# Where a convolution stage takes its spectrum's sign and mean, in which banks its last unit works, and in which order its first unit is built

## The chip, the cores and the metric

The kernel runs on one core of one Trainium2 chip. The metric is the device time of one execution in microseconds. Before the change it was 3066.25 us, the median of 3 runs (3065.99 to 3067.99).

## What is computed

The input `x` has 8 images of 32 channels of 256 x 256. Four layers follow one another, each of the form `x = x + layer(groupnorm(x))`. Only the first two matter here, and the normalisation between them:

```python
# _gn: mean and variance over pairs of channels of one image
# layer 0: a Fourier layer: 64 x 32 modes are mixed over channels, then inverted
x_ft = jnp.fft.rfft2(x)
out_lo = jnp.einsum('bixy,ioxy->boxy', x_ft[:, :, :M1H, :M2H], w1)
out_hi = jnp.einsum('bixy,ioxy->boxy', x_ft[:, :, -M1H:, :M2H], w2)
...
out = jnp.fft.irfft2(out_ft, s=(h, w))
x = x + (out + bias)
# layer 1: one 5 x 5 filter, the same for all channels
x = x + conv5x5(_gn(x))
```

Layers 2 and 3 are a recurrence over the columns and a mix of directional maxima; the change does not touch them.

## The kernel before

The program has four stages, one after another: `forward_and_mix` (forward transform and mixing of modes, which leaves the mixed spectra in the DRAM tensor `smd`), `inverse_and_conv` (inverse transform, residual sum, 5 x 5 convolution, which leaves layer 1's result in the DRAM tensor `x2d`), `recurrence` and `maxima_and_mix`. All the change lies in `inverse_and_conv` (L297 to L664). That stage starts at about 295 us and ends at about 1034 us of the profiled execution.

**Units.** The stage works on 16 units `u`. A unit is half an image, 16 channels; two units share one image `b` and so one spectrum. A unit's channels are held as two halves `ch`, each of 4 groups, so a unit has 8 groups `g`. The loop from L614 runs over units and, inside, over groups. The order in each engine's queue is the order in which this loop issues instructions, since the whole stage is under a manual schedule; nothing reorders it.

**What one unit needs before its convolution.** These steps run for unit u+1 and u+2 in between the groups of unit u:

- `load_spectrum(b)` (L345): three DMAs bring a spectrum from `smd` to a tile `spec`. From the third image on they are issued from ScalarE's queue, in odd units after group 2 (L652).
- `spectrum(b)` (L355): VectorE negates one half of the tile (L358, 64 x 1024 elements in place), TensorE takes the mean of the image with one matmul into a bank `y0` (L360, two passes), and six small VectorE instructions (L362 to L372) turn that mean into a correction of the spectrum's row 0 (L371) and into statistics. It is called for image 0 before the loop, for image 1 in unit 0 after group 2 (L635), and for images 2 to 7 in odd units 1, 3, 5, 7, 9 and 11 after group 5 (L654).
- `over_rows(u, c)` (L394): four matmuls (L401, recorded as 8) into a bank `tp`, then a ScalarE copy into SBUF (L408). Inside the loop these run after groups 3 to 6 for unit u+2.
- `over_columns` through `transform(u, p)` (L410, L579): matmuls of one of 9 column blocks `p` into two banks `up` (L418, recorded as 16), then two VectorE sums with the input into the tiles `x1` (L427). After blocks 2, 5 and 8 GpSimd issues the loads of the next unit's input (L379). There are five tiles `x1`, used in turn by halves of units, so block 0 of unit u+2 writes to tiles that held the last half of unit u-1 and the first half of unit u.
- `squares` (L435): sums of squares per group, by ScalarE (L444) or, where told, VectorE (L440). `scale(u, ch)` (L446): matmuls of these sums (L451), one VectorE instruction (L455), and a power by GpSimd (L457), which gives the factor `r` that the convolution's results of that half are multiplied with.

**The convolution of a group** (`conv`, L469): 18 matmuls (L487, recorded as 36) into three banks `vp`, then five VectorE instructions (L520) that multiply the banks by `r` and add them to `x1` in place, then ScalarE's squares (L527). After a half of a unit, `store` (L534) writes it to `x2d` by 12 DMAs from the queue of SyncE (for the last half of all, half of them from ScalarE's). `statistics(u-1)` (L550) after group 2 takes the sums over partitions with four matmuls (L556, recorded as 8) into a bank, then four VectorE instructions (L564 to L568) and a GpSimd power (L569).

**Banks.** The eight banks of PSUM are shared out by tag: `vp` has 4, `up` has 3, `st` has 1. The one bank `st` serves `y0`, `tp`, the sums of `scale` and those of `statistics` in turn: each has to wait until the one before has been read. A group of `conv` takes 3 of the 4 `vp` banks.

**The start of the stage** (L594 to L613): after the first spectrum, `over_rows` of unit 0 uses `st` and `up` in turn; then the 9 blocks of unit 0 are built with the `vp` banks, and `over_rows` of unit 1 stands after blocks 1, 3, 5 and 7, always in the bank `st`. The squares of blocks 5 to 8 are taken by ScalarE for half 0 and by VectorE for half 1. `scale(0, 1, 3)` comes next in TensorE's queue, then block 0 of unit 1, then unit 0's convolution with `scale(0, 0, 3)` within its first group.

**The end of the stage.** In the last unit there is nothing left to transform; only conv groups, their squares and two small sums remain. The next stage begins with a transpose of statistics (L707) into SBUF that the stage's tiles have held.

Of the kernel before, what the change touches and what calls it, by code (L numbers as in the profile page):

```python
# [16 lines left out]
P = 128  # L17
# [10 lines left out]
NT = 9  # L28
# [268 lines left out]
def inverse_and_conv(tc, k, d, smd, xmean, x2d, stb, first):  # L297
# [13 lines left out]

    PLACES = (1, 2, 3, 5, 6, 7, 8)
    with ExitStack() as ctx:
        one = ctx.enter_context(tc.tile_pool(name="a2c", bufs=1))
# [39 lines left out]

        def spectrum(b):  # L355

            t = specs[b]
            nc.vector.tensor_scalar_mul(t[64:128, :, 1], t[64:128, :, 1], -1.0)  # L358
            y0 = ps.tile([P, C], F32, name=f"y0_{b}", tag="st")
            nc.tensor.matmul(y0, lhsT=k.dc, rhs=t[:, :, 0, 0], start=True, stop=True)  # L360
            yb = sm.tile([P, C], F32, name=f"yb_{b}", tag="yb")
# [107 lines left out]
        def conv(u, ch, g, between=()):  # L469
# [3 lines left out]


            vps = [
                ps.tile([P, 2 * (hi - lo), Q], F32, name=f"vp_{u}_{ch}_{g}_{lo}", tag="vp", bufs=4) for lo, hi in BANKS
            ]
# [71 lines left out]

        def statistics(u):  # L550
            b, h = units[u]
            s1 = state.pop(u)["s1"]
            n8 = 2 * G
            sp = ps.tile([P, 2, n8], F32, name=f"s2_{u}", tag="st")
            for n in range(4):
                nc.tensor.matmul(  # L556
                    sp,
                    lhsT=k.valid[:, 2 + min(n, 2), :],
                    rhs=s1[:, :, n].rearrange("p k c g -> p k (c g)"),
                    start=n == 0,  # L560
                    stop=n == 3,
                )
            st = sm.tile([P, 2, n8], F32, name=f"st2_{u}", tag="st2")
            nc.vector.tensor_copy(st, sp)  # L564
            ve = sm.tile([P, n8], F32, name=f"ve2_{u}", tag="ve2")
            nc.vector.tensor_tensor(ve, st[:, 0], st[:, 0], ALU.mult)
            nc.vector.tensor_tensor(ve, st[:, 1], ve, ALU.subtract)
            nc.vector.tensor_scalar(ve, ve, 0.0, EPS, ALU.max, ALU.add)  # L568
            nc.gpsimd.tensor_tensor(st[:, 1], ve, k.mhalf[:, :n8], ALU.pow)  # L569
            return st  # L570

# [21 lines left out]
        with tc.manual_schedule(engines=None):  # L593
            load_spectrum(0)  # L594
            load_spectrum(1)
            for i in range(3):
                load(0, i)
            spectrum(0)
            for u in range(2):
# [3 lines left out]
            for p in range(NT):  # L603
                transform(0, p)
                if p % 2:
                    over_rows(1, p - 1)
                if p == 4:
                    for ch in range(2):
                        squares(0, ch, 1, 1, 5)
            for ch in range(2):  # L610
                squares(0, ch, 2, 5, NT, ch == 1)
            scale(0, 1, 3)
            transform(1, 0)  # L613
            for u in range(n):  # L614
                more, beyond = u + 1 < n, u + 2 < n
                for g in range(2 * G):
# [10 lines left out]
                    if g == 2 * G - 1 and beyond:  # L627
                        transform(u + 2, 0)
                    if g == 1 and u > 0:
                        scale(u, 1)  # L630
                    if g == 2:
                        if u > 0:
                            st = statistics(u - 1)
                        elif beyond:
                            spectrum(units[u + 2][0])  # L635
                    if g == G - 1 and beyond:
# [3 lines left out]
                    if g == 6 and more:  # L640
                        squares(u + 1, 0, 2, 8, NT)
                    squares2(u, g // G, g % G)
                    if g == 1 and more:
                        for ch in range(2):
                            squares(u + 1, ch, 0, 0, 1)
# [4 lines left out]
                    if u % 2 and u + 3 < n:  # L650
                        if g == 2:
                            load_spectrum(units[u + 3][0])  # L652
                        elif g == 5:
                            spectrum(units[u + 3][0])  # L654
                    if g % G == G - 1 and (u, g) != (n - 1, 2 * G - 1):
# [544 lines left out]
```

## Time and profile before

| | before |
|---|---|
| median of 3 runs | 3066.25 us |
| profiled execution | 3069.01 us |
| its span | 3067.2 us |
| TensorE busy over the span | 2796.5 us (91%) |
| VectorE busy | 2585.2 us (84%) |
| ScalarE busy | 1870.4 us (61%) |
| GpSimd busy | 858.2 us (28%) |

Times inside the profiled execution are counted from the start of its span. In lines of the timeline, the columns are start in us, length in us, engine, source line, operation, the tile written and the tiles read, shape, count, and in square brackets how long the engine sat idle before it and what ended that. One row may merge many instructions of one kind. In lines of windows, the columns are the window, its length, then for each engine the busy us and the number of instructions, then granted TensorE clock, DMA share and GB/s.

Almost all of the stage's time lies between the first and last L520 instruction, 357.29 and 1021.18 us, and can be cut into units there: a unit's length is taken from the start of its first L520 instruction to that of the next unit's. Read so from the timeline of VectorE, the lengths of units 0 to 14 are 40.49, 42.31, 41.35, 45.51, 41.35, 45.55, 41.35, 45.48, 41.35, 42.31, 41.35, 42.31, 41.35, 41.35 and 37.59 us.

### The profile page before, as it was taken

How to read it: one execution, taken by the hardware profiler on the slowest of the kernel's cores; microseconds unless marked ns; L12 is line 12 of the kernel's file. 1: busy time of each engine (PE TensorE's matmuls, PEld its weight loads, DVE VectorE, ACT ScalarE, POOL GpSimd, SP SyncE). 2: the span in 40 equal slices, each digit the busy share in tenths (PEclk: the TensorE clock that was granted, in tenths of full speed). 3: DMA queues.
4: the chain of work that ended last, by engine and by line, in shares of the span. 5: the costliest groups of instructions: out<-in, count | busy, mean ns of one | idle time of the engine just before them, and what ended most of it. 6: DMA issues, size and time to landing. Idle time of an engine off the chain costs nothing.

```text
span 3067.2 us, 111686 instructions
## 1 busy us (share of the span) xinstructions
PE 2796.5 (91%) x47736; PEld 1645.3 (54%) x47736; DVE 2585.2 (84%) x5178; ACT 1870.4 (61%) x4482; POOL 858.2 (28%) x1247
## 2 busy tenths in 40 slices
PE   7986799999999799999999999999999588888887
PEld 4665344444444466666666666666666233333333
DVE  5752587778888589999999999999999799999997
ACT  3432377676777578888888888888887222222222
POOL 0110011111111355555555555555555200000000
PEclk9985899999999899999999999999999799999998
DMA  9977577777775565667666676666764588888885
GB/s 385 392 283 222 154 230 225 218 224 219 231 221 165 146 148 139 142 158 167 148 142 141 154 167 151 144 142 149 167 157 115 180 327 329 328 330 329 330 327 226
DMA packets 468193, 655.69 MB, mean 214 GB/s; under 512 B 328784, under 2 KB 329696, under 8 KB 441456
## 3 DMA queue, kind: packets, MB, share of 16 engines
q1 hardware_dynamic: 407528, 487.89, 54.6%
q0 software_dynamic: 16784, 84.11, 8.4%
q10 hardware_dynamic: 43384, 76.55, 6.9%
q8 instruction: 374, 6.13, 0.8%
q14 instruction: 123, 1.01, 0.1%
HBM read 371.63 MB, written 272.63 MB: 210 GB/s over the span
## 4 chain that ended last, share of the span: by engine, by line
PE 69%; DVE 20%; DMA 5%; issue 3%; ACT 2%; SPq 0%; ACTq 0%; POOL 0%; DVEq 0%; POOLq 0%
PE r L753 14%; PE z L753 13%; PE vp L487 11%; PE ni L753 6%; PE nh L753 6%; PE up L418 4%; DVE rv L1012 4%; PE yp L131 3%; DMA spec<-smd 3%; DVE dq L1018 2%; DVE uq L1020 2%; DVE m L1026 2%; DVE m L1024 2%; DVE m L1022 2%; PE sp L158 2%
## 5 line engine op out<-in xcount | busy, mean ns | idle before, releaser
L761 PE MATMUL z<-hs,weights 64*64 64x256 f32 x4080 | 539.2, 382 | 0.0
L761 PE MATMUL ni<-hs,weights 64*64 64x256 f32 x4080 | 525.7, 375 | 0.0
L761 PE MATMUL r<-hs,weights 64*64 64x256 f32 x4080 | 525.0, 375 | 0.0
L843 POOL TENSOR_TENSOR xw<-xw,hs 128x256 f32<-128x256 f32 x496 | 340.2, 686 | 635.3 <-DVE hs L842 635.3
L1058 ACT ACTIVATE ot<-o,bres 128x512 f32<-128x512 f32 x256 | 155.1, 688 | 505.1 <-PE o L1043 489.7
L487 PE MATMUL vp<-x,c_conv 64*64 64x384 f32 (+5 forms) x4608 | 428.8, 491 | 4.9 <-DVE x L520 4.9
L520 DVE SCALAR_TENSOR_TENSOR x<-vp,r,x 128x128 f32<-128x128 f32 (+2 forms) x640 | 350.6, 563 | 87.9 <-PE vp L487 75.1
L837 POOL TENSOR_TENSOR a<-zm,xn 128x256 f32<-128x256 f32 x510 | 373.1, 732 | 7.0 <-ACT zm L830 6.7
L835 ACT ACTIVATE n<-n,bih 128x256 f32<-128x256 f32 x510 | 259.5, 509 | 186.4 <-DVE n L834 186.4
L1043 PE MATMUL o<-m,wsc 32*32 32x512 f32 x3072 | 228.8, 724 | 108.0 <-DVE m L1026 104.4
L753 PE MATMUL r<-hs,weights 64*64 64x256 f32 x2040 | 318.9, 389 | 4.4 <-DVE hs L842 3.4
L753 PE MATMUL z<-xn,weights 64*64 64x256 f32 x2040 | 305.8, 377 | 14.9 <-DMA xw<-x2d 14.9
L487 PEld LDWEIGHTS vp<-x,c_conv 64*64 64x64 f32 x4608 | 222.4, 132 | 180.0 <-issue 104.4
L753 PE MATMUL r<-xn,weights 64*64 64x256 f32 x2040 | 305.3, 376 | 2.1 <-ACT rs L828 2.1
L753 PE MATMUL nh<-xn,weights 64*64 64x256 f32 x2040 | 306.2, 377 | 0.0
L753 PE MATMUL z<-hs,weights 64*64 64x256 f32 x2040 | 305.3, 376 | 0.0
L753 PE MATMUL ni<-hs,weights 64*64 64x256 f32 x2040 | 305.1, 375 | 0.0
L733 ACT ACTIVATE xn<-xw,shift,turned 128x256 f32<-128x256 f32 x496 | 290.3, 586 | 0.0
L829 DVE SCALAR_TENSOR_TENSOR n<-nh,bhh,rs 128x256 f32<-128x256 f32 x510 | 246.2, 483 | 46.4 <-ACT rs L828 32.6
L761 PEld LDWEIGHTS ni<-hs,weights 64*64 64x64 f32 x4080 | 284.8, 133 | 0.3
L761 PEld LDWEIGHTS r<-hs,weights 64*64 64x64 f32 x4080 | 280.9, 131 | 0.2
L828 ACT ACTIVATE rs<-r,brz 128x256 f32<-128x256 f32 x510 | 241.7, 474 | 54.2 <-PE r L761 33.8
(162 smaller groups left out, 6230.3 us busy)
## 6 DMA issues: line engine op xcount, KB each, us to landing
xb<-in_xl_dram POOLq DMA_DIRECT2D x96, 768.0 KB, 7.6
xa<-in_xt_dram SPq DMA_DIRECT2D x64, 1024.0 KB
x<-x3d SPq DMA_DIRECT2D x32, 2048.0 KB
fw<-fwd SPq DMA_DIRECT2D x32, 2048.0 KB
out_dram<-ot ACTq DMA_DIRECT2D x64, 1024.0 KB
xw<-x2d SPq DMA_DIRECT2D x248, 256.0 KB
fwd<-fm SPq DMA_DIRECT2D x248, 256.0 KB
x3d<-xw SPq DMA_DIRECT2D x248, 256.0 KB
```

The lines of the kernel that those rows point to most:

```text
L487: ins = nc.tensor.matmul(vps[bank][to, :, dst], lhsT=k.conv[r, P : P + 64] if kind == 2 else k.conv[r, o], rhs=pair_of(u, ch, g, lo, hi, s ...
L520: nc.vector.scalar_tensor_tensor(x, src[o], r1[rows, g : g + 1], x, ALU.mult, ALU.add, accum_out=s1[rows, 0, n, ch, g : g + 1])
L733: nc.scalar.activation(norms[bi][:, b, w], raws[bi][:, b, w], AF.Identity, bias=shift[:, b : b + 1], scale=sc[:, 1, b : b + 1])
L753: ins = nc.tensor.matmul(out[r], lhsT=weights[r, kind, gate, :], rhs=src[r], start=start, stop=stop)
L761: ins = nc.tensor.matmul(out[pairs[1 - i]], lhsT=weights[r, kind, gate, :], rhs=prev[r, :, q0 : q0 + Q], start=False, stop=stop,)
L828: rs = nc.scalar.activation(r, p["r"], AF.Sigmoid, bias=brz[:, 0:1])
L829: nc.vector.scalar_tensor_tensor(m, p["nh"], bhh[:, 2:3], r, ALU.add, ALU.mult)
L835: nc.scalar.activation(m, m, AF.Tanh, bias=bih[:, 2:3])
L837: product = nc.gpsimd.tensor_tensor(a, zm, cur, ALU.mult)
L843: nc.gpsimd.tensor_tensor(raw, raw, new, ALU.add)
L1043: nc.tensor.matmul(pts[b2][i][32 * j : 32 * j + 32].rearrange("p (w q) -> p w q", q=Q), lhsT=wsc[q, b2, t, :], rhs=src[j][q, b2], start=first,
L1058: nc.scalar.activation(ot[:, i], pts[b2][i], AF.Identity, bias=bres[:, b2, i : i + 1])
```

## The change

1. `spectrum` is split in three: `turn(b, engine)` is the sign, `means(b, y0)` the matmul, `spectrum(b, y0)` the rest. For images 2 to 7 the sign is issued on GpSimd, in the even unit that follows the load, after group 0. The mean's matmul goes into columns 16 to 47 of the bank that `statistics` uses after group 2 of that even unit, ahead of the statistics' own matmuls, and the six VectorE instructions follow those of the statistics. The call after group 5 of odd units is gone. Images 0 and 1 keep VectorE's sign and a bank `y0` of their own.
2. In the last unit, odd groups of `conv` take their three banks from `up`, even groups from `vp` as before.
3. In the first unit, `over_rows` of unit 1 stands after blocks 1, 3, 4 and 7 instead of 1, 3, 5 and 7, and all but the first use `up` banks. VectorE takes the last squares of half 0 and ScalarE those of half 1, the other way round than before. `scale(0, 1, 3)` moves from before unit 0's convolution to after its group 1, where `scale(u, 1)` of all other units stands.

```diff
+    FIRST = (1, 3, 4, 7)
...
-        def spectrum(b):
-
+        def turn(b, engine):
             t = specs[b]
-            nc.vector.tensor_scalar_mul(t[64:128, :, 1], t[64:128, :, 1], -1.0)
-            y0 = ps.tile([P, C], F32, name=f"y0_{b}", tag="st")
-            nc.tensor.matmul(y0, lhsT=k.dc, rhs=t[:, :, 0, 0], start=True, stop=True)
+            engine.tensor_scalar_mul(t[64:128, :, 1], t[64:128, :, 1], -1.0)
+
+        def means(b, y0=None):
+
+            if y0 is None:
+                y0 = ps.tile([P, C], F32, name=f"y0_{b}", tag="st")
+            nc.tensor.matmul(y0, lhsT=k.dc, rhs=specs[b][:, :, 0, 0], start=True, stop=True)
+            return y0
+
+        def spectrum(b, y0):
+
+            t = specs[b]
...
+            tag, bufs = ("up", 3) if u == len(units) - 1 and g % 2 else ("vp", 4)
             vps = [
-                ps.tile([P, 2 * (hi - lo), Q], F32, name=f"vp_{u}_{ch}_{g}_{lo}", tag="vp", bufs=4) for lo, hi in BANKS
+                ps.tile([P, 2 * (hi - lo), Q], F32, name=f"vp_{u}_{ch}_{g}_{lo}", tag=tag, bufs=bufs)
+                for lo, hi in BANKS
             ]
...
-        def statistics(u):
+        def statistics(u, new=None):
...
-            sp = ps.tile([P, 2, n8], F32, name=f"s2_{u}", tag="st")
+            both = ps.tile([P, 2 * n8 + C], F32, name=f"s2_{u}", tag="st")
+            sp = both[:, : 2 * n8].rearrange("p (k n) -> p k n", k=2)
+            if new is not None:
+                means(new, both[:, 2 * n8 :])
...
+            if new is not None:
+                spectrum(new, both[:, 2 * n8 :])
             return st
...
-            spectrum(0)
+            turn(0, nc.vector)
+            spectrum(0, means(0))
...
-                if p % 2:
-                    over_rows(1, p - 1)
+                if p in FIRST:
+                    i = FIRST.index(p)
+                    over_rows(1, 2 * i, *(("up", 3) if i else ("st", 1)))
...
-                squares(0, ch, 2, 5, NT, ch == 1)
-            scale(0, 1, 3)
+                squares(0, ch, 2, 5, NT, ch == 0)
             transform(1, 0)
...
-                    if g == 1 and u > 0:
-                        scale(u, 1)
+                    if g == 1:
+                        scale(u, 1, 2 if u else 3)
                     if g == 2:
                         if u > 0:
-                            st = statistics(u - 1)
+                            st = statistics(u - 1, units[u + 2][0] if beyond and u % 2 == 0 else None)
                         elif beyond:
-                            spectrum(units[u + 2][0])
+                            new = units[u + 2][0]
+                            turn(new, nc.vector)
+                            spectrum(new, means(new))
...
+                    if g == 0 and u and u % 2 == 0 and beyond:
+                        turn(units[u + 2][0], nc.gpsimd)
...
-                        elif g == 5:
-                            spectrum(units[u + 3][0])
```

## The prediction

> **What bounds the kernel now.** I read the page first, for the stage, then the windows of the convolution stage, then TensorE's timeline in its three parts. In the windows (a steady stretch, the last unit, and the start):
>
> ```profile
> 814.00:856.00 42.00, 41.31 (x486) 19.68 (x482) 34.59 (x108) 30.79 (x96) 7.11 (x10) 1.00 0.86 240
> 982.00:1024.00 42.00, 34.33 (x344) 20.06 (x342) 28.43 (x107) 26.40 (x80) 9.85 (x11) 0.99 0.58 155
> 335.00:352.00 17.00, 9.49 (x90) 3.34 (x90) 8.50 (x19) 9.59 (x26) 3.15 (x5) 0.77 0.64 234
> ```
>
> The second number pair is TensorE: full in the steady stretch (41.31 of 42 us), not in the last unit (34.33 of 42) nor at the start (9.49 of 17). So in the middle only TensorE's work and its stops count; VectorE (34.59) and GpSimd (7.11) have room. In TensorE's timeline a full group is 3.16 us of conv (L487, 36 records), 1.02 of L418 and 1.01 of L401, start to start: 5.19 us, with no gap.
>
> Stops in the middle, at L360 in unit 1, then in unit 3 on TensorE and VectorE:
>
> ```profile
> 425.46 1.08 PE L401 MATMUL tp<-c_eh,spec 128*64 128x256 f32 x8
> 427.23 0.42 PE L360 MATMUL y<-spec,c_dc 128*128 128x32 f32 x2 [0.69 <-ACT tt L408]
> 427.58 3.23 PE L487 MATMUL vp<-x,c_conv 64*64 64x256 f32 x36
> ...
> 517.10 1.08 PE L401 MATMUL tp<-c_eh,spec 128*64 128x256 f32 x8 [1.62 <-DVE yb L362]
> ...
> 516.13 0.69 DVE L358 TENSOR_SCALAR spec<-spec 64x1024 f32<-64x1024 f32 x1 [4.67 <-DMA spec<-smd]
> ```
>
> The mean's matmul waits until ScalarE has emptied the one `st` bank, so L401 to L360 takes 1.77 us instead of 1.01. In unit 3 the spectrum also lands late: VectorE stands 4.67 us before the sign, and behind it wait the conv results and the next `tp`.
>
> At the start and in the last unit:
>
> ```profile
> 341.39 1.98 PE L401 MATMUL tp<-c_eh,spec 128*64 128x256 f32 x8 [3.65 <-ACT tt L408]
> 343.30 1.54 PE L418 MATMUL up<-tt,c_gw 64*32 64x512 f32 x16
> 344.76 0.61 PE L451 MATMUL v<-sq,c_valid 128*128 128x4 f32 x4
> 349.23 0.59 PE L451 MATMUL v<-sq,c_valid 128*128 128x4 f32 x2 [3.85 <-DVE junk L440]
> 349.75 1.96 PE L418 MATMUL up<-tt,c_gw 64*32 64x512 f32 x16
> 351.64 3.56 PE L487 MATMUL vp<-x,c_conv 64*64 64x256 f32 x24
> ...
> 1003.55 3.65 PE L487 MATMUL vp<-x,c_conv 64*64 64x384 f32 x36 [0.64 <-DVE x L520]
> 1007.83 3.65 PE L487 MATMUL vp<-x,c_conv 64*64 64x384 f32 x36 [0.64 <-DVE x L520]
> 1012.11 3.65 PE L487 MATMUL vp<-x,c_conv 64*64 64x384 f32 x36 [0.64 <-DVE x L520]
> ```
>
> At the start TensorE waits 3.65 us for the `st` bank and 3.85 us for VectorE's squares, and everything queues behind. In the last unit it waits in each group for VectorE to free a `vp` bank: a period of 4.28 us where conv alone is 3.16. And the stage's end is a transfer, the last store:
>
> ```profile
> 1034.23 0.98 DVE L707 STREAM_TRANSPOSE turned<-stb 128x768 f32<-128x768 f32 x1 [8.40 <-DMA x2d<-x]
> ```
>
> **What the Trainium skill says.** GPSIMD Engine Reference, section "Elementwise — side-by-side cycle accounting": some 1.03 cycles per element for port-bound bodies and 2.6 for two inputs, at 1.2 GHz. The same page, "Specifications": its SBUF interface is shared with VectorE, and clashes with instructions that read two SBUF inputs or run in a two-port mode. The trace has two-input GpSimd instructions of 256 elements at 686 to 732 ns, 2.7 to 2.9 ns an element, which is above the page's 2.6 cycles (2.2 ns); no one-input instruction of size is shown. TensorE: Matmul & The Clock Gate, "What's actually happening": the clock is halved after an idle window of about 3.4 us. The clock record agrees: 0.5 from 340.9 to 344.3 and 347.7 to 354.5, beside these waits. DMA: Bandwidth & Descriptors, "Issuing engines are not separate DMA queues": all transfers interleave on the same 16 engines, which matters for the late spectra.
>
> **Part 1, spectra 2 to 7.** Removed from odd units: by the unit lengths against the undisturbed 41.35 us, 0.96 us in units 1, 9 and 11 and 4.16, 4.20 and 4.13 in units 3, 5 and 7. Sum 15.4 us. Unit 13, odd and without a spectrum, is 41.35, so nothing else in odd units is left.
> Added to six even units: two matmul records ahead of the statistics'. These run eight in 1.00 us, 0.125 each, so 0.25; at L360 the two took 0.35. I take 0.3, six times: 1.8 us, on TensorE's path. They wait for no bank the statistics did not wait for.
> VectorE: six instructions, 1.16 us long in unit 1 (428.56 to 429.72). Here they follow the statistics, where VectorE then stands idle for 1.31 us before L427 of block 4 (idle ahead of 412.80). That covers them, and the first `tp` that needs them begins 3.6 us after the statistics end. If the cover were gone, L427 and L520 would slip by up to 1.2 us, six times 7 us at most.
> GpSimd: one sign of 1024 elements. Estimate from the page 0.9 to 2.2 us, from the trace's two-input rate 2.9; I take 2. It is issued after group 0 and needed by `tp` after group 3, some 17 us later; the deadline stands whichever value holds, so cost nothing; below nothing is excluded, since nobody waits for its end. It waits for the spectrum's landing: at the latest seen, 516.1, against about 524 for its turn, so 8 us spare. Behind it in GpSimd's queue are the next two input loads (used a unit later) and the power of `scale(u, 1)`, after group 1, needed by group 4: 14 us spare. SBUF clash: L520 and L427 read one operand from PSUM and one from SBUF, so I count none; at worst 2 us of VectorE six times, in slack.
> With the stops gone, what is late next in units 3, 5 and 7? SyncE's queue: its store DMAs stop from 506.76 to 516.12, until the spectrum lands, and go on to 519.5. Block 0 of unit 5 overwrites that tile, and now does so about 39.4 us into the unit, at 520.8 to 521.4; the store's queue falls quiet by about 521. Cost 0 to 0.5 us, three times; I take 0.
> Sum: 15.4 - 1.8 = 13.6 us gained; bounds 10 (cover partly gone, stores late) and 14.2.
>
> **Part 2, last unit.** With six banks in turn TensorE runs at 3.16 us a group; VectorE needs 3.0 (five L520 with their accumulator reads, 1005.34 to 1008.34), ScalarE about 2. Groups 0 and 1 start at 985.85 and 989.0; then `scale(15, 1)` waits, as now, for ScalarE's squares (its last records at 994.14), so group 2 starts at 994.46 as before. It ends at 997.6, the statistics take 1.0, and groups 3 to 7 at 3.16 each end at 1014.4 against 1019.0: 4.6 us. The last store then begins at about 1016.6 instead of 1021.2. But the half before it and the reads of `first` keep the DMA engines at 0.98 busy from 1005 to 1015 and at work until 1017.5, having started less than 1 us earlier; so I give back 0.5: 4.1 us; bounds 2 and 4.6.
>
> **Part 3, first unit.** I lay the new order out with the old durations. Blocks go at VectorE's pace, 1.28 us each for two L427, or TensorE's (0.95, plus 1.01 where a `tp` stands). The waits for `st` are gone: `tp` for blocks 3, 4 and 7 find free `up` banks. Block 2 at 328.9 as now; block 4 at 331.9, 5 at 333.9, 6 at 334.9, 7 at 336.0, 8 at 338.3 instead of 343.3; its L427 end at 340.8. ScalarE: squares of blocks 1 to 4 from 334.7 to 340.7 (8 x 0.755), then the last `tp` copy to 341.35, for which unit 1's block 0 waits: 341.4 to 342.5 (343 at half clock). Conv begins then, at 342.5 to 343, instead of 351.64. VectorE's squares of half 0 end at 343.7, before `scale(0, 0)` asks for them (344.7 or later), so no stop. From conv's start to the first L520 everything is as before (5.65 us). So 8.6 to 9.1 us earlier; less `scale(0, 1)` after group 1, 6 records, 0.76 us, now on TensorE's path: 8.2 gained. Half clock for the first group costs 1.3, and was paid before too; bounds 6.5 and 10.
>
> **Sum.** 13.6 + 4.1 + 8.2 = 25.9 us. From the profiled execution, 3069.01: 3043.1. From the median, 3066.25: 3040.4. The profiled execution is 2.8 us above the median: either profiling's own, or one late spectrum less in the timed runs (3.2 us), which then have less to gain. I stand between: 3041 us.
>
> **Rivals.**
> - *Less to gain:* the late landings of units 3, 5 and 7 are chance of the profiled run. Without them part 1 gains 6 x 0.96 - 1.8 = 4.0, and the whole 4.0 + 4.1 + 8.2 = 16.3: 3050. For it, the 2.8 us above; against it, three landings of nearly equal lateness (4.16, 4.20, 4.13) and runs within 2 us of each other. Or the last store is bound by its transfers alone: 4.1 less, 3045.
> - *More:* the half clock of 347.7 to 354.5 (6.8 us, so 3.4 of loss) is avoided and the last store moves in full (0.5): 29.8 us, 3036.
> - *Slower:* the stores. Units without stops reach block 0 of unit u+2 earlier, while SyncE's stores still wait behind a late spectrum; VectorE then waits in L427 for the tile, and conv behind it. It decides from a landing later than about 35 us into an odd unit (now 34.7 at the latest), and costs a us for each us beyond. To be slower by 0.2% it must eat 26 us and 6 more, 5.3 in each of six units: 3073 and up. Against it, the loads and stores keep their places in the queues.
> - *Not what it says:* the built order shows the six signs on GpSimd, `up` banks in the last unit's odd groups, the new start; this rival is void. That the hidden waits were all hidden anyway (no change, 3066) is against TensorE's full rows.
>
> **Chances.** Forecast, 3036 to 3046: 0.72. Less to gain, 3046 to 3059: 0.18. More, under 3036: 0.06. No change: 0.015. Slower: 0.025. The range 3035 to 3050 leaves about 0.17 out, on both sides together. A measurement of this kernel tells 0.2%, about 6 us, from no change: faster 0.96, same 0.015, slower 0.025.
>
> **What would show it.** Unit lengths read from L520: odd units at 41.35, even units from 2 to 12 at 41.6 to 41.7; no wait of `tp` for VectorE's `yb`; six GpSimd instructions of 1 to 3 us. Conv's first record near 342.5, the first L520 near 348. In the last unit a period of 3.2 us, and VectorE's transpose some 4 us sooner after group 0 of that unit. It would be wrong if VectorE waits on `x2d` stores in the middle, if even units grow by more than 0.5 us, or if the last store takes as much longer as it starts earlier.

## The result and the profile after

| | before | after |
|---|---|---|
| median beside each other | 3067.12 us (3065.99 to 3070.75) | 3046.77 us (3042.76 to 3054.56) |
| ratio of the two | | 0.993, interval 0.9915 to 0.9945 |
| profiled execution, its span | 3069.01, 3067.2 us | 3042.76, 3041.0 us |
| first result of the convolution (VectorE) | 357.29 us | 347.29 us |
| sum of units 1 to 13 | 552.9 us | 542.0 us |
| last unit, first to last of these instructions | 32.92 us | 27.63 us |
| transpose that opens the next stage | 1034.23 us | 1008.63 us |

By the ratio, the change makes the kernel faster by 21.5 us, 17 to 26 by the interval. The forecast was 3041 with a range of 3035 to 3050; the time lies inside, 5.8 us above the forecast. The profiled execution is the fastest of the four runs; why the others are up to 12 us slower is what most of the experiments below are about. Lines named L498, L531, L436 and L364 are those that were L487, L520, L427 and L360 before.

First the windows of the kernel after: the same steady stretch as before, the last unit, and the start. The columns are window, length, busy us and instructions of TensorE, its weight loads, VectorE, ScalarE and GpSimd, then clock, DMA share and GB/s.

```profile
814.00:856.00 42.00, 42.00 (x496) 20.11 (x492) 34.30 (x108) 30.81 (x95) 10.54 (x13) 1.00 0.86 244
967.00:996.00 29.00, 25.28 (x288) 16.04 (x278) 22.98 (x87) 20.64 (x61) 9.29 (x10) 1.00 0.73 194
325.00:342.00 17.00, 14.83 (x196) 4.79 (x200) 11.52 (x19) 12.29 (x39) 2.61 (x5) 1.00 0.48 166
```

TensorE's 41.31 of 42 us have become 42.00: no stop is left in this stretch. GpSimd went from 7.11 to 10.54; 2.77 of that is the moved sign. In the last unit TensorE is busy for 25.28 of 29 us where it was for 34.33 of 42, and at the start for 14.83 of 17 where it was for 9.49, at full clock instead of 0.77.

The start and the last unit in TensorE's timeline of the kernel after:

```profile
341.91 1.09 PE L427 MATMUL up<-tt,c_gw 64*32 64x512 f32 x16 [1.48 <-ACT tt L417]
342.94 2.23 PE L498 MATMUL vp<-x,c_conv 64*64 64x256 f32 x24
345.10 0.83 PE L460 MATMUL v<-sq,c_valid 128*128 128x4 f32 x6
...
973.58 0.38 PE L460 MATMUL v<-sq,c_valid 128*128 128x4 f32 x2 [1.76 <-ACT junk L453]
973.89 3.23 PE L498 MATMUL vp<-x,c_conv 64*64 64x256 f32 x36
977.05 1.06 PE L570 MATMUL s<-s,c_valid 128*128 128x16 f32 x8
978.04 15.21 PE L498 MATMUL vp<-x,c_conv 64*64 64x256 f32 x180
```

The waits of 3.65 and 3.85 us at the start are one of 1.48, and the convolution begins at 342.94 instead of 351.64. In the last unit the gaps of 0.64 us in each group are gone: five groups (180 records) run in 15.21 us, 3.04 each. What stays is 1.76 us for ScalarE's squares.

The mean of a new spectrum, in the same timeline of the kernel after, unit 2:

```profile
439.16 1.09 PE L427 MATMUL up<-tt,c_gw 64*32 64x512 f32 x16
440.18 0.42 PE L364 MATMUL s<-spec,c_dc 128*128 128x32 f32 x2
440.42 1.04 PE L570 MATMUL s<-s,c_valid 128*128 128x16 f32 x8
```

It costs 0.24 us from its start to that of the statistics' matmuls, with no wait ahead of it.

Then the stage's end, from VectorE's timeline:

```profile
1008.63 0.98 DVE L726 STREAM_TRANSPOSE turned<-stb 128x768 f32<-128x768 f32 x1 [8.64 <-DMA x2d<-x]
```

It stands behind the last store as before, 13.29 us after the last result of the convolution (13.04 before).

Read by units, from VectorE's timeline, units 0 to 14 are now 40.86, 41.41, 41.51, 41.35, 41.57, 41.35, 41.58, 41.35, 41.57, **44.55**, 41.45, 41.35, 41.57, 41.35 and 37.58 us. All odd units stand at 41.35 but unit 1 (41.41) and unit 9, and this one is new. VectorE's timeline there, in the kernel after:

```profile
759.03 0.68 DVE L436 TENSOR_TENSOR x<-up,xb 128x512 f32<-128x512 f32 x1
763.78 0.69 DVE L436 TENSOR_TENSOR x<-up,xb 128x512 f32<-128x512 f32 x1 [4.07 <-ACT junk L453]
```

These two are block 0 of unit 11. The second writes the tile that unit 9's first half was held in, so it has to wait for that half's store. The releaser that the profile names, ScalarE's squares, had long been done; a transfer is behind it. SyncE's queue, which issues the store, and GpSimd's, in the same execution:

```profile
744.27 0.47 SPq L552 DMA_DIRECT2D x2d<-x  x1
754.30 0.31 SPq L556 DMA_DIRECT2D x2d<-x  x1
...
756.01 0.40 SPq L557 DMA_DIRECT2D x2d<-x  x1
```
```profile
754.75 1.12 POOL L388 DMA_DIRECT2D xb<-in_xl_dram  x2 [13.71 <-DVE x L436]
759.20 1.03 POOL L466 TENSOR_TENSOR r<-ve,c_mhalf 128x4 f32<-128x4 f32 x1 [3.33 <-DVE ve L464]
760.33 2.77 POOL L358 TENSOR_SCALAR spec<-spec 64x1024 f32<-64x1024 f32 x1
```

SyncE stands from 744.74 to 754.30 in the middle of the store and issues its last five DMAs until 756.41. GpSimd meanwhile issues two input loads of 768 KB. The shares that the three queues' packets took of the 16 DMA engines, us by us, worked out from the trace's packets:

```
from    input load  store  spectrum
751       0.00      0.58     0.34
752       0.00      0.20     0.49
753       0.00      0.00     0.20
754       0.00      0.00     0.00
755       0.00      0.47     0.00
756       0.88      0.00     0.00
757       1.01      0.00     0.00
758       0.94      0.07     0.00
759       0.61      0.40     0.00
760       0.50      0.53     0.00
761       0.83      0.19     0.00
762       0.60      0.35     0.00
763       0.00      0.96     0.00
```

The store goes on when the spectrum's last packets are through (753 to 754). Then the input load takes the engines almost alone from 756 to 759 and shares them after that; its last packet ends at 763.38, and the store's last transfer lands at 763.56. VectorE goes on at 763.78 and conv behind it at 765.16. I call this a *store stop*. It costs unit 9 its 3.2 us.

### The profile page after: what moved, and what is told of

The parts are those of the page before. It is cut to its first block, busy times and chain, and to the rows that moved or that the text cites. A ratio compares the mean times of both kernels' runs of the same rounds, so it can differ in the third digit from the quotient of the medians.

```text
span 3041.0 us, 111672 instructions
## 1 busy us (share of the span) xinstructions
PE 2787.3 (92%) x47736; PEld 1644.8 (54%) x47736; DVE 2580.6 (85%) x5172; ACT 1868.2 (61%) x4482; POOL 874.4 (29%) x1253
## 3 DMA queue, kind: packets, MB, share of 16 engines
q14 instruction: 123, 1.01, 0.1%
## 4 chain that ended last, share of the span: by engine, by line
PE 71%; DVE 20%; issue 4%; DMA 3%; ACT 1%; SPq 0%; POOL 0%; ACTq 0%; DVEq 0%; POOLq 0%
PE r L772 14%; PE z L772 13%; PE vp L498 13%; PE ni L772 7%; PE nh L772 6%; PE up L427 4%; DVE rv L1031 4%; PE yp L131 3%; DVE dq L1037 2%; DVE uq L1039 2%; DVE m L1045 2%; DVE m L1043 2%; DVE m L1041 2%; PE sp L158 2%; PE tp L410 2%
## 5 line engine op out<-in xcount | busy, mean ns | idle before, releaser
L531 DVE SCALAR_TENSOR_TENSOR x<-vp,r,x 128x128 f32<-128x128 f32 (+2 forms) x640 | 350.6, 563 | 90.5 <-PE vp L498 78.2
L498 PE MATMUL vp<-x,c_conv 64*64 64x384 f32 (+5 forms) x4608 | 422.1, 490 | 2.4 <-DVE x L531 2.4
L498 PEld LDWEIGHTS vp<-x,c_conv 64*64 64x64 f32 x4608 | 221.7, 132 | 172.6 <-issue 93.8
```

Source lines behind the costliest of these rows:

```text
L498: ins = nc.tensor.matmul(vps[bank][to, :, dst], lhsT=k.conv[r, P : P + 64] if kind == 2 else k.conv[r, o], rhs=pair_of(u, ch, g, lo, hi, s ...
L531: nc.vector.scalar_tensor_tensor(x, src[o], r1[rows, g : g + 1], x, ALU.mult, ALU.add, accum_out=s1[rows, 0, n, ch, g : g + 1])
```

## The experiments

Theory S: what the prediction's sum lacks are store stops. They come from late spectra, differ in number from run to run, and take back most of what part 1 removes. The rivals: the moved steps themselves cost more (GpSimd's sign, the mean in the statistics' bank), or parts 2 and 3 give less than their sums.

The kernel before spreads over 18 us on the chip of the first comparison (3061.36 to 3079.33 in 51 runs), so all ratios below are against runs of the kernel before in the same comparison, whose medians were 3069.55, 3069.72 and 3066.47 us. The changed kernel has two ratios, 0.993 from the first result and 0.9945 from the run below. Differences from it are counted from 0.9945; from 0.993 they would move by 4.6 us. So a difference of a few us isn't shown by the times alone, and the lengths of units in the traces have to carry it.

**The changed kernel once more.** No edit.

> The changed kernel as it is, to see how its executions spread on one chip beside the parts alone. Theory S (a store that is held up behind a late spectrum stops VectorE in L436 of an odd unit, about 3.2 us each time, in a number of units that differs from run to run): times lie at about 3039.5 us plus a multiple of some 3.2 us, 3042 to 3055, and the profiled execution shows odd units of about 44.5 us beside those of 41.35. Rival N (the spread is noise that has nothing to do with this stage): no odd unit over 41.5 us, and a spread as before, 3 to 5 us, without such units.

Measured: 3053.15 us (3046.3 to 3055.71, 6 runs), ratio 0.9945 (0.9926 to 0.9963). The profiled execution took 3055.11 us, with three store stops: units 1, 3 and 11 are 44.69, 46.25 and 44.20 us, and unit 4 43.04. VectorE's waits in it, from 350 to 985 us:

```profile
DVE x L436 <- PE up L427: 16.9, 15, 3.7
DVE x L436 <- DMA x2d<-x: 5.8, 1, 5.8
DVE x L436 <- ACT junk L453: 4.2, 1, 4.2
```

The columns are us in total, times, and the longest. Here the profile names the store itself as the releaser of 5.8 us. In the kernel after, the same view has `DVE x L436 <- PE up L427` with 13.2 us, 14 times, so 1.3 at the longest is usual: the 3.7 of this run is a third stop, in unit 11, with a wrong releaser. The last unit is 29.32 us instead of 27.63, for another reason, in TensorE's timeline:

```profile
983.83 0.39 PE L460 MATMUL v<-sq,c_valid 128*128 128x4 f32 x2 [1.75 <-ACT junk L453]
984.15 4.92 PE L498 MATMUL vp<-x,c_conv 64*64 64x256 f32 x36
```

The same 36 records took 3.23 us above; the clock was 0.5 from 984.5 to 987.9. To the end of conv this execution is 11.9 us behind the one of the result: 9.2 by stops, 1.7 by the clock in the last unit, 1.0 by a later start. So S has its stops, but not of one size. With their effect on the next unit, those in units 1 and 11 cost 3.2 and 2.7 us. The one in unit 3 cost 6.4, and there the clock also fell to 0.5, from 523.7 to 527.1 us.

**One part at a time.** Each is the kernel before with one part of the change.

```diff
 # part 1, with means() and turn() of the change
-            nc.vector.tensor_scalar_mul(t[64:128, :, 1], t[64:128, :, 1], -1.0)
+                    if g == 0 and u and u % 2 == 0 and beyond:
+                        turn(units[u + 2][0], nc.gpsimd)
-                            st = statistics(u - 1)
+                            st = statistics(u - 1, units[u + 2][0] if beyond and u % 2 == 0 else None)
-                        elif g == 5:
-                            spectrum(units[u + 3][0])
```

> Only part 1 (sign by GpSimd, mean in the statistics' bank, even units); the start and the last unit as before. Theory: even units 2 to 12 at 41.57 us, odd ones at 41.35 but for those that theory S stops; 15.4 us of stops less 6 x 0.22, so about 14 us faster than before, less 3.2 for each stopped unit: 3052 to 3062, ratio 0.996 to 0.998 in the median. Rival (the old stops were chance of one run): under 5 us faster.

Measured: 3067.35 us (3058.83 to 3078.45, 14 runs), ratio 0.9992 (0.9979 to 1.0005). That is some 2 us, and zero lies inside the interval. In its profiled execution odd units are 41.35, but unit 3 is 45.77 and unit 7 45.01, with units 4 and 8 at 42.83 and 42.78; VectorE's longest waits at the sum of block 0 (L435 in this kernel) are 5.3 and 4.4 us. Those four units give back 10.5 us. The expected ratio of 0.996 to 0.998 was missed: this is the part that fell short. By the number the rival of this run came true (under 5 us), but not by its reason: late spectra were no chance of one execution. In the profiled executions of parts 2 and 3 below, where the middle is as before, odd units with a spectrum hold 8.1 and 11.5 us above 42.31, if in part in other units.

```diff
 # part 2
-                ps.tile([P, 2 * (hi - lo), Q], F32, name=f"vp_{u}_{ch}_{g}_{lo}", tag="vp", bufs=4) for lo, hi in BANKS
+            tag, bufs = ("up", 3) if u == len(units) - 1 and g % 2 else ("vp", 4)
```

> Only part 2 (odd groups of the last unit in the up banks). Theory: the last unit's conv ends 5.3 us earlier as in the trace of the changed kernel, and the last store moves with it in full: 5.3 us faster, 3061 to 3062. Rival (the transfers at the stage's end take back what starts earlier): 0 to 2 us faster. Odd units as before: 42.3 or 45.5 us with a spectrum.

Measured: 3062.75 us (3058.41 to 3072.0, 22 runs), ratio 0.9981 (0.9972 to 0.999), some 6 us, as expected. In its profiled execution the last unit is 29.26 us with half clock from 998.6 to 1002.0, so 3.7 us are gained there, where the full clock gives 5.3.

```diff
 # part 3
-                if p % 2:
-                    over_rows(1, p - 1)
+                if p in FIRST:
+                    i = FIRST.index(p)
+                    over_rows(1, 2 * i, *(("up", 3) if i else ("st", 1)))
...
-                squares(0, ch, 2, 5, NT, ch == 1)
-            scale(0, 1, 3)
+                squares(0, ch, 2, 5, NT, ch == 0)
-                    if g == 1 and u > 0:
-                        scale(u, 1)
+                    if g == 1:
+                        scale(u, 1, 2 if u else 3)
```

> Only part 3 (the other order of the first unit). Theory: first L520 at about 347.3 us instead of 357.3, unit 0 longer by 0.4: 9.6 us faster, about 3057. Rival (unit 0 or the units after it give part of it back, as loads and stores do not come earlier): 5 us or less. Sum of the three parts, by the theory, equal to the whole change.

Measured: 3059.64 us (3051.95 to 3070.39, 22 runs), ratio 0.997 (0.9961 to 0.998), some 9 us, as expected. The first result of the convolution is at 348.29 and the clock is full there. The three ratios multiplied give 0.9943; the whole gave 0.9945. So within the intervals the parts don't hinder each other, and parts 2 and 3 are not what is missing.

**The spectrum's load earlier.** If the stops come from late spectra, an earlier load removes them. It moves from odd units, after group 2, to the even unit before, after group 6, and from ScalarE's queue to SyncE's.

```diff
-            queue = nc.scalar if b > 1 else nc.sync
+            queue = nc.sync
...
-                    if u % 2 and u + 3 < n:
-                        if g == 2:
-                            load_spectrum(units[u + 3][0])
+                    if u % 2 == 0 and u + 4 < n and g == 6:
+                        load_spectrum(units[u + 4][0])
```

> The changed kernel with the load of spectra 2 to 7 moved: from odd units after group 2 (ScalarE's queue, just ahead of a store) to the even unit before, after group 6 (SyncE's queue, behind a store's last issue and one and a half units ahead of the next tile that a store could hold up). Same work. Theory S (a slow spectrum holds SyncE's store, and that store holds x1's tile and VectorE's L436 in odd units): no odd unit above 41.6 us, no wait of L436 for x2d, TensorE never idle for 2 us in the middle; compared with the changed kernel 3 us less for each unit that stopped, 5 to 12 us in the median, ratio to before 0.990 to 0.992, and a narrower spread. Rival N (spread and shortfall come from elsewhere): as the changed kernel, ratio about 0.9945.

Measured: 3042.75 us (3041.05 to 3045.4, 5 runs), ratio 0.9919 (0.9905 to 0.9933). Odd units 1 to 13 are 41.35 or 41.36 us, even units 41.57, and the runs lie within 4.4 us. This is the whole view of what VectorE waited for at L436, from 350 to 985 us:

```profile
DVE x L436 <- PE up L427: 13.2, 14, 1.3
```

No store, no wrong releaser, nothing over 1.3 us. The run keeps all three parts of the change, so the steps that they move are not the cause by themselves, and S stands. By the times alone this would be less sure: the interval overlaps that of the first result, 0.9915 to 0.9945. Load time and queue were changed together; they were not tried apart.

**The same load one group later.** The dose in the other direction.

```diff
-                        if g == 2:
+                        if g == 3:
```

> The changed kernel with the load of spectra 2 to 7 one group later (after group 3 of odd units instead of 2, 7.4 us), so that it goes out together with the store of the unit's first half. Theory S: the store's last issues come some 5 to 8 us later, so VectorE waits in L436 at the end of nearly every odd unit with a spectrum, 5 to 10 us each: 30 to 60 us slower than the changed kernel. Rival (the store isn't held by the spectrum, since GpSimd uses the spectrum only in the next unit): within 3 us of the changed kernel.

Measured: 3080.95 us (3079.89 to 3086.69, 5 runs), ratio 1.0041 (1.0027 to 1.0056): some 29 us slower than the changed kernel, just under the range expected. But the stop is not where I expected it. The six odd units with a load are 47.2 to 49.8 us, and the time goes between groups 5 and 6 (11.1 to 13.7 us instead of 5.19), while no store keeps VectorE waiting at L436. ScalarE's timeline in unit 3:

```profile
501.98 0.47 ACTq L351 DMA_DIRECT2D spec<-smd  x1
502.49 1.31 ACTq L353 DMA_DIRECT2D spec<-smd  x1
502.77 0.19 ACT L538 ACTIVATION_READ_ACCUMULATOR junk<-x 128x1 f32 x1
503.83 10.35 ACTq L353 DMA_DIRECT2D spec<-smd  x1
514.23 0.59 ACT L417 COPY tt<-tp 128x512 f32<-128x512 f32 x1 [11.28 <-issue]
```

The third issue of the load takes 10.35 us, and ScalarE, which issues it, can't copy `tp` meanwhile; TensorE then waits for it in `tp`, 29.4 us over six times; by each of these waits the clock fell to 0.5, for 3.4 or 6.8 us. So this run shows that a spectrum's load is dear in the wrong place. It does not show that more lateness gives longer store stops, and for that link it decides nothing. The kernel after has the same issue at 485.65 with 5.24 us, where nothing waited for ScalarE.

**The sign on VectorE.** The rival that GpSimd's sign is dear.

```diff
-                        turn(units[u + 2][0], nc.gpsimd)
+                        turn(units[u + 2][0], nc.vector)
```

> The changed kernel with the sign on VectorE at the same place (even units after group 0) instead of GpSimd. My prediction took GpSimd's sign for free and VectorE for slack: by that, no difference (0 to 1 us, within the spread), since VectorE's 0.69 us after group 0 falls into its idle time before the next conv results. Rival: what gained was GpSimd's taking over 0.69 us of VectorE's time six times: 4 us slower than the changed kernel, even units at 42.2 us.

Measured: 3049.13 us (3048.04 to 3055.8, 4 runs), ratio 0.9943 (0.9925 to 0.9961) against 0.9945 with GpSimd. No difference is seen, but these intervals are 5 us to either side and couldn't tell the rival's 4 us from none. The units can: even ones are 41.5 to 41.6 us but for those behind a stop, and not the rival's 42.2. Store stops stand in units 1, 3, 7 and 9 of the profiled execution. So GpSimd's sign isn't their cause, and in this place the engine of the sign is worth nothing either way.

**The mean in a bank of its own.** The rival about the shared bank: here the mean's matmul comes after the statistics and takes `st` for itself.

```diff
-            if new is not None:
-                means(new, both[:, 2 * n8 :])
...
-                spectrum(new, both[:, 2 * n8 :])
+                spectrum(new, means(new))
```

> The changed kernel with the mean in a bank st of its own after the statistics', instead of in theirs. Theory (the one st bank is what made the old mean stop TensorE): its matmul waits until VectorE has read the statistics, and VectorE reads them only after L436 of block 3, so TensorE stops for 1 to 2 us in each of six even units: units of 42.5 to 43.5 us, 6 to 12 us slower than the changed kernel. Rival (the gain came only from moving the mean away from group 5): even units at 41.6 us, no difference.

Measured: 3067.26 us (3054.91 to 3077.61, 12 runs), ratio 0.9992 (0.9979 to 1.0005), some 14 us behind the changed kernel and more than the 6 to 12 expected. Its even units 2 to 12 are 44.79, 44.74, 44.69, 43.17, 44.72 and 43.18 us, 15.9 us in sum over 41.57. TensorE's timeline of this kernel in unit 2:

```profile
443.17 1.07 PE L568 MATMUL s<-s,c_valid 128*128 128x16 f32 x8
445.65 0.42 PE L364 MATMUL y<-spec,c_dc 128*128 128x32 f32 x2 [1.41 <-DVE st L576]
445.99 3.13 PE L498 MATMUL vp<-x,c_conv 64*64 64x256 f32 x24
```

The mean waits 1.41 us until VectorE has emptied the bank, and behind it 24 records take 3.13 us where 36 take 3.23 at full clock. In four of the six units the clock was at 0.5 for 3.4 us afterwards, which is the other half of their 3.2 us; the other two cost 1.6. So the bank that the mean shares with the statistics is worth about 14 us in this place, and the step of part 1 that priced it (six times 0.3 us) holds.

**Block 0 moved away from the store.** If the link between late store and stop is the tile of block 0, then block 0 later in the order ends the stops, with the load where it was.

```diff
-                    if g == 2 * G - 1 and beyond:
-                        transform(u + 2, 0)
...
+                    if g == 1 and u and more:
+                        between.append(lambda: transform(u + 1, 0))
```

> The changed kernel with block 0 of the unit after next moved from the end of a unit (after group 7) into group 1 of the next unit, some 7 us later; loads and stores stay where they are. It tells which link of theory S stops VectorE. If it is the tile x1 that a held-up store still reads, VectorE's L436 finds the tile free by then: no odd unit over 42 us, although SyncE's queue still stands still behind late spectra; time as with the early load, ratio about 0.992. Rival (the late spectrum stops the unit by another way: GpSimd's sign, its queue, or the transfers' crowding): odd units of 44 to 46 us stay, ratio about 0.9945.

Measured: 3053.47 us (3052.59 to 3055.99, 4 runs), ratio 0.9956 (0.9941 to 0.997). Odd units are 42.17 and even ones 42.39 throughout, so no stop at all, and the runs lie within 3.4 us. But the traced execution doesn't test the link, since it had no late spectrum. Five of its six spectra were through 22.4 to 23.6 us into their units, the sixth at 32.6.

How late is late can be read from five traces with the load and block 0 in their old places: the kernel after, its second execution, part 1, the sign on VectorE and the mean in a bank of its own. They have 30 odd units with a spectrum. In ten of them there was a stop, and there the spectrum's last packet ended 33.8 to 35.0 us into the unit and SyncE went on with the store within 1 us of it. In the other twenty it ended at 21.2 to 32.1, and none stopped. Five of the ten stops cost 2.7 to 3.3 us; the other five, behind which the clock fell to 0.5 for 3.4 us, cost 4.9 to 6.4.

So the link from a late spectrum to a stop is shown by these units and by the earlier load. That it goes by the tile is shown less directly: what stands is the sum that writes a tile under store, and the profile named the store as the releaser of 5.8 us above, and of 4.4 us in part 1.

The time with block 0 later is no better, since the order has a price of its own, 0.82 us in each unit (11 us in all): VectorE now waits at L436 for TensorE 28 times for 27.0 us, instead of 14 times for 13.2.

**The earlier load in the kernel before.** How much of the gain is the load's alone?

```diff
-            queue = nc.scalar if b > 1 else nc.sync
+            queue = nc.sync
...
+                    if u % 2 == 0 and u + 4 < n and g == 6:
+                        load_spectrum(units[u + 4][0])
```

> The kernel before, with the load of spectra 2 to 7 moved to the even unit before, after group 6, on SyncE's queue; nothing else. It tells how much of part 1's gain an earlier load alone would have given. Theory (late landings cost what is over 0.96 us): all odd units with a spectrum at 42.3 us, so per execution the sum of what they have over that is gained: 9.6 us by the profile before, more on this chip, where units of 45.3 to 45.7 were four: 8 to 15 us faster, ratio 0.995 to 0.997. Rival (the stops have another cause than the landing): odd units of 45 us stay, no gain.

Measured: 3060.96 us (3056.75 to 3063.27, 12 runs), ratio 0.9984 (0.9974 to 0.9993), some 5 us, less than expected. All units with a spectrum are 42.30 or 42.31 us; the 4.1 to 4.2 us of units 3, 5 and 7 are gone down to 0.96. By these times the late landings of the kernel before cost a usual run some 5 us, 2 to 8 by the interval. The three profiled executions with that middle hold 9.6, 8.1 and 11.5 us of them. Whether profiled executions have more of them than others, or the earlier load costs something elsewhere, is not known.

**The best version.** The earlier load, and in the last unit `scale(15, 1)` between the banks of group 2 instead of ahead of it, since TensorE waited there 1.75 us for ScalarE.

```diff
-                    if g == 1:
+                    if g == 1 and more:
                         scale(u, 1, 2 if u else 3)
+                    if g == 2 and not more:
+                        between.append(lambda: scale(u, 1))
 # and the earlier load as above
```

> The changed kernel with the early load, and in the last unit the sums of scale(15, 1) moved from after group 1 into group 2, so that TensorE doesn't stand 1.75 us before group 2 for ScalarE's squares (and doesn't fall to half clock, 1.6 us more in some runs). Theory: conv's end 2 us earlier than with the early load alone where that kept its clock, 3.6 where not: about 3039 to 3041 on this chip, ratio about 0.991. Rival (ScalarE's squares or the last store are then next and take it back): ratio as with the early load, 0.992.

Measured: 3038.12 us (3035.94 to 3039.87, 4 runs), ratio 0.9904 (0.9889 to 0.9919): 29 us faster than the kernel before by this ratio. From the earlier load alone (0.9919) it isn't clear by time; the last unit shows the difference. TensorE's timeline in its last unit:

```profile
971.18 0.61 PE L460 MATMUL v<-sq,c_valid 128*128 128x4 f32 x4
971.72 1.50 PE L498 MATMUL vp<-x,c_conv 64*64 64x384 f32 x12
973.15 1.06 PE L570 MATMUL s<-s,c_valid 128*128 128x16 f32 x8
974.14 15.20 PE L498 MATMUL vp<-x,c_conv 64*64 64x256 f32 x180
```

No wait stands ahead of L460, and five groups in 15.20 us are those of the full clock. The last unit is 25.99 us, against 27.63 in the kernel after and 29.30 in the kernel with the earlier load alone.

## Why the prediction came out as it did

The whole came within the range, and parts 2 and 3 came about as argued. In part 1 the waits that were to go did go, but most of their gain came back as another wait: one term, taken as zero, was too small. That the total is only 5.8 us above the forecast is in part luck, since part 3 gave more than its sum. Point by point, from the profiled execution of before to that of after (25.85 us to the end of conv, 26.2 in the span):

- *Part 1, 13.6 us.* Units 1 to 13 gave 10.9. The 15.4 us of waits in odd units did go. Even units grew by 0.22 us (group 2 to 3 takes 7.63 instead of 7.40), not 0.3: 0.5 us better in sum. What failed is the step on the stores: "the store's queue falls quiet by about 521. Cost 0 to 0.5 us, three times; I take 0". Unit 9's spectrum landed 34.5 us into the unit, no later than the 34.7 in the kernel before. The store's last DMA was issued soon after, 36.6 us into the unit, as I had assumed. But it landed at 43.7; the input load had most of the DMA engines in between. The prediction had looked at the queue's issues, not at what their transfers share. In the profiled execution that was 3.2 us once; in others up to four stops of 2.7 to 6.4 us. The rival "slower" had the right mechanism, and its deciding point (a landing at 35 us) was too late by at least half a us.
- *Part 1 in a usual run.* Its sum was two things: 6 x 0.96 - 1.8 = 4.0 us of certain gain, and 9.6 us of late landings. The rival "less to gain" took the second for chance, and it was partly right: what comes and goes is how many spectra are late, and in which units. Part 1 alone measured some 2 us; with the earlier load the whole of the change gains 0.0081, 25 us, and of this 0.0016 (5 us) is the load's own, as the kernel before with the earlier load shows. The late landing was not removed by part 1: the wait was moved from VectorE's sign to block 0 of the unit after next. All these are differences of intervals of some 4 us to either side, so the 2 us are no more than "little".
- *Six small VectorE instructions and GpSimd's sign, each at nothing.* Right. Even units would show them. The sign took 2.77 us, near the upper bound of 2.9; I had taken 2. GPSIMD Engine Reference, section "Elementwise — side-by-side cycle accounting", of the Trainium skill, has 1.03 cycles an element for port-bound bodies; an estimate from it is 0.9 us. The trace has 2.7 ns an element, no less than with two inputs; the measurement decides.
- *Part 2, 4.6 less 0.5.* The last unit gave 5.29, since a group takes 3.04 us and not 3.16 where groups follow each other with no other work between them; five times 0.12 is 0.6 of the 0.7 that it gave beyond 4.6. Of the 0.5 given back for the last store only 0.25 were (13.29 against 13.04 us from conv's end to the transpose). In executions where the clock drops in this unit it is 3.6 to 3.7.
- *Part 3, 8.2 us.* It gave 9.6: 10.0 at the first result, less 0.37 in unit 0. Conv's first record was forecast for 342.5 to 343 and came at 342.94. From there to the first result it took 4.35 us instead of the 5.65 that I kept, because the clock was full (the first 24 records took 2.23 us instead of 3.56): just the 1.3 us that I had named as the price of half clock "paid before too". `scale(0, 1)` cost 0.37 and not 0.76. That part of the rival "more" came true. The stage itself began 1.4 us later in this execution (the mean of image 0 at 316.63, 315.22 before), so counted from there the gain is 11.4 at the first result.
- *From the profiled execution to the median.* I stood between 3043.1 and 3040.4. The sum from the profiled execution met the profiled execution of after (3042.76), but its errors cancelled there: 2.7 too much in part 1, 0.9 and 1.4 too little in parts 2 and 3. That the median run is slower than this one because it has more stops is likely: the second execution of the same kernel had three, and half clock in the last unit besides. The other timed runs were not traced.

What stays open: why the same spectrum lands later in some runs than in others. That SyncE's issue stands still until a load from another engine's queue has landed is read from times that fall together (753 to 754 with 754.30 here, 516.12 with 516.13 before, and the ten units above); what holds it was not taken apart. SyncE also stands for 2 to 4 us in the stores of units without a spectrum. A sixth tile for the halves was not tried.

## What to carry to other kernels

A wait that is removed from an engine may have kept a later buffer reuse safe from a slow transfer: for a step that lets an engine reach a tile earlier, ask when the last transfer from that tile lands, with all that shares the DMA engines then, and not when it is issued. If the profiled execution holds waits of varying size for a transfer, split the forecast into the fixed part and the part that comes and goes, and move the transfer first. An experiment that takes the suspected lateness away (an earlier load) tells more than one that adds to it, which may hit another queue.

## What the runs showed of the hardware

- *An issue can hold its engine.* The first DMA issue of a spectrum on ScalarE's queue took 0.47 us in unit 3. The third took 5.24 us there in the kernel after, and 10.35 with the load a group later, and during these two ScalarE computed nothing (it was idle for 5.73 and 11.28 us). SyncE stood for 9.6 us in the middle of a store.
- *A transfer can starve beside a large one.* DMA: Bandwidth & Descriptors, section "Issuing engines are not separate DMA queues", of the Trainium skill, says that transfers from all engines interleave on the same 16 engines. The trace agrees, but the shares were far from even: 0.88 to 1.01 for the input load and 0.00 to 0.07 for the store from 756 to 759 us.
- *A wait of 1.75 us can be enough to halve the clock, and its place in time decides.* TensorE: Matmul & The Clock Gate, section "What's actually happening", has half clock after an idle window of some 3.4 us, with windows that run freely. Such windows show in the traces: within one execution the clock changes at times that lie multiples of 3.41 us apart (984.5 is 134 of them after 527.1). Eight traced executions wait for 1.75 or 1.76 us in the same place of the last unit. In four of them the whole wait lay within one of these windows, and the 36 records behind it took 4.86 to 4.92 us. In the other four a window ended during the wait, so that at most 1.67 us of it lay within one, and the same records took 3.23. The six waits of 1.41 us for the mean in a bank of its own part in the same way: the clock fell behind the four that had at least 1.37 us within one window, and not behind the two that were cut about in half. So a window need not be idle throughout, and the length of a wait alone doesn't tell: 1.37 us were enough in one place where 1.67 were not in the other. This is the window of the kernel with the earlier load, one of the first four, with 0.51 in the clock's column:

```profile
975.00:978.50 3.50, 3.50 (x26) 2.10 (x29) 0.16 (x1) 3.34 (x12) 1.01 (x1) 0.51 0.80 181
```

TensorE counts as busy for all 3.50 us of it, which is why a share of busy time doesn't show the loss.
